# A decoder layer on one core: the key weights of groups 1 and 2 loaded with the initial loads

## The chip, the core and the metric

The kernel runs on one core of a Trainium2 chip. The core has a matrix engine (TensorE, in the profile PE, with its weight loads as PEld), three engines for elementwise work (VectorE or DVE, ScalarE or ACT, GpSimd or POOL) and SyncE (SP), which here only issues DMAs. The engines run side by side; each works through its own instructions in order and waits for others by semaphores. DMAs issued from SP and ACT move data between the chip's memory (HBM) and the on-chip memory (SBUF), or inside SBUF. Matrix products land in PSUM, in banks of 128 x 512 numbers.

The metric is the device time of one execution, in microseconds; the median of several runs counts. All data are 32-bit floats.

## The reference

One layer of a decoder on 1024 tokens of width 512, batch 1. Attention has 32 query heads and 8 key and value heads (groups) of 128 numbers, with rotary position factors and a causal mask; then a feed-forward part of width 1792. Each half is followed by a layer norm.

```python
q, k, v = x @ wq, x @ wk, x @ wv            # 32, 8 and 8 heads of 128
q = q * cos + rotate_half(q) * sin          # k likewise
k, v = repeat(k, 4), repeat(v, 4)           # four query heads share a group
att = softmax(where(causal, q @ k.T / sqrt(128), -inf))
x = layernorm(x + (att @ v) @ wo)
n = x * rsqrt(mean(x * x) + 1e-5) * ln_w
x = layernorm(x + (silu(n @ gate.T) * (n @ up.T)) @ down.T)
```

## The kernel before

**Stages.** A short opening loads x (transposed, in blocks a11, a12, a21, a22), rotary tables and the first weights, and projects the queries and keys of group 0 and the first half of its values. Then eight groups follow, one after the other (`for g in range(KV)`), and last the feed-forward part. In a group the scores of 32 strips of 32 tokens x 4 heads are taken in an order by row tiles of 128 tokens, ORDER = 7, 1, 5, 3, 4, 2, 6, 0. A strip goes through `scores`: products on TensorE into a pair of PSUM banks, mask and lowest value on DVE (L603), exp on ACT (L620), reciprocal on DVE (L624), scaling on ACT (L625), a turn of 32 x 32 blocks on DVE (L628). The part of a strip's tile p that the mask leaves empty is cleared on POOL (L618). When the four strips of a row tile are there, `gather` has SP issue 16 DMAs (L678) that bring the turned blocks into place ("moved<-turned"), and later TensorE multiplies them with the values (tile o).

**What fills the gaps.** Between the scores of group g TensorE does the projections of group g + 1. `steps` is the list of their weights: step 0 is the keys of groups 1 and 2, step 1 queries 4 and 5, step 2 queries 6 and 7, step 3 the values of groups 2 and 3, and so on. `project_two` makes two projections at once by a Strassen-like scheme of seven half-size products; it needs sums of the weight's blocks, which `weigh` makes on POOL (L268 to L270, and one more at L541).

**Loading a step.** `load(s)` issues the DMA of a step's weights on SP (L228), and for keys it adds a scaling of the whole weight on POOL (L236). Step 0 is loaded when the second query head of group 0 has been projected for the second half of the tokens, step 1 after the fourth (in `project_queries`), and step s + 2 at the end of `project_two(s)`. The weights lie in `two_rows`, a pool of four buffers of 128 x 1024; at the start it holds the weights of queries 0 and 1, of queries 2 and 3, and the two parts of the output weight of group 0.

**The queries' buffer.** `held_q` has three places; queries of group g and half `even` lie in place (2g + even) mod 3. Group 0 uses places 0 and 1; place 2 is first written by `project_two(1)`, with the queries of group 1.

**Order.** TensorE's instructions stand in the order in which they are written. On the other engines a planner sets the order by its own estimate of times; `tc.issue_after(ins)` puts an instruction behind another of the same engine. Every DMA on SP also waits for the DMA eight places before it to have landed, since eight semaphores are used in turn.

## Time and profile before

| | |
|---|---|
| runs | 1273.88 us median of 3 (1272.79 to 1274.13) |
| profiled execution | 1272.16 us, span 1270.4 us |
| mean granted TensorE clock | 0.995 of full speed |
| TensorE matmul | busy 1249.0 us, 98% of the span |
| TensorE weight load | busy 737.3 us, 58% |
| DVE | busy 884.4 us, 70% |
| ACT | busy 466.2 us, 37% |
| POOL | busy 469.1 us, 37% |
| DMA queue of SP and ACT | 35.2% of sixteen engines |

How to read the views: a row of a timeline gives start and duration in us, the engine, the line, the operation with its output and input tile, how many instructions are merged, and in brackets the engine's idle time before it and what ended that. SPq is the part of SP that issues DMAs; its row gives the time of issuing, not of the transfer. A row of waits gives the waiting engine, line and tile, who released it, the total in us, how often, and the longest. A row of stretches gives, for a window of the span, the window's length, then each engine's busy time and its number of instructions, the granted TensorE clock (PEclk), the share of DMA engines in use and GB/s. Line L135 is the helper that records every matmul, so matmuls are told apart by their tiles: s scores, o products with the values, q_ps, k_p and q_p projections, y the output projection.

### The profile page before, as it was taken

The numbers are of one execution on the slowest core, as the hardware profiler recorded it, in microseconds if no ns is written. First come the engines' busy times: TensorE is split into PE (matmuls) and PEld (weight loads), VectorE is DVE, ScalarE is ACT, GpSimd is POOL, SyncE is SP. The second block draws the span as 40 slices with busy tenths as digits, with TensorE's granted clock in tenths as the row PEclk, the third lists the DMA queues.
The fourth block names the chain that finished last, engine by engine and source line by source line (L and its number), as shares of the span: only waits on it lengthen the run. The fifth ranks groups of instructions, "written<-read, shape, count | busy, mean of one in ns | idle before, by whom it ended". The sixth has DMA issues, their size and how long they took to land. (4 is left out here: it accounts for less than half of the span.)

```text
span 1270.4 us, 14265 instructions
## 1 busy us (share of the span) xinstructions
PE 1249.0 (98%) x4142; PEld 737.3 (58%) x4142; DVE 884.4 (70%) x1821; ACT 466.2 (37%) x922; POOL 469.1 (37%) x708
## 2 busy tenths in 40 slices
PE   9989999999999999999999999999999999999998
PEld 5644576565556755655567556554656744444887
DVE  4657787788788767878787678687765664436743
ACT  0433344444443444344444444455555111111000
POOL 3442333433434233425341323253320756543321
PEclk9999999999999999999999999999999999999999
DMA  7243225433543344334433433544443711110000
GB/s 257 48 104 91 74 67 136 114 77 80 137 111 86 83 125 98 94 82 119 102 85 85 132 79 81 133 112 111 99 98 90 213 34 50 50 34 1 17 17 34
DMA packets 89326, 115.55 MB, mean 91 GB/s; under 512 B 18464, under 2 KB 60192, under 8 KB 89248
## 3 DMA queue, kind: packets, MB, share of 16 engines
q1 hardware_dynamic: 88240, 112.66, 35.2%
q10 hardware_dynamic: 1008, 1.97, 0.4%
q8 instruction: 34, 0.56, 0.2%
q14 instruction: 44, 0.36, 0.1%
HBM read 37.23 MB, written 2.10 MB: 31 GB/s over the span
## 5 line engine op out<-in xcount | busy, mean ns | idle before, releaser
L620 ACT ACTIVATE p<-s,low 128x928 f32<-128x928 f32 (+31 forms) x256 | 179.0, 699 | 361.5 <-DVE low L603 346.8
L135 PE MATMUL o<-moved,v 128*128 128x512 f32 x550 | 255.1, 597 | 0.0
L628 DVE STREAM_TRANSPOSE turned<-p 128x1024 f32<-128x1024 f32 (+7 forms) x244 | 186.8, 775 | 97.7 <-ACT p L625 62.5
L625 ACT ACTIVATE p<-p,share 128x928 f32<-128x928 f32 (+31 forms) x256 | 187.3, 735 | 121.5 <-DVE share L624 121.5
L603 DVE CUSTOM_DVE_ANT_0 s<-s,mask 128x928 f32<-128x928 f32 (+31 forms) x256 | 179.1, 700 | 63.9 <-PE s L135 63.0
L135 PE MATMUL s<-k,queries 128*128 128x512 f32 (+15 forms) x576 | 204.1, 464 | 2.3 <-ACT p L620 2.3
L135 PEld LDWEIGHTS s<-k,queries 128*128 128x128 f32 x576 | 108.6, 191 | 108.4 <-issue 96.3
L135 PEld LDWEIGHTS o<-moved,v 128*128 128x128 f32 x550 | 102.9, 191 | 104.5 <-issue 98.9
L135 PE MATMUL q_p<-blocks,wq 128*128 128x512 f32 x260 | 123.7, 594 | 0.0
L433 POOL TENSOR_TENSOR queries<-queries,q_b 128x512 f32<-128x512 f32 x52 | 71.0, 1365 | 124.9 <-DVE queries L432 118.5
L618 POOL MEMSET p<- 128x96 f32 (+2 forms) x192 | 26.0, 151 | 213.6 <-DVE turned L628 187.7
L135 PE MATMUL y<-wo,oT 128*128 128x256 f32 x428 | 103.8, 381 | 0.0
L135 PEld LDWEIGHTS y<-wo,oT 128*128 128x128 f32 x428 | 79.8, 190 | 21.5 <-issue 7.4
L427 DVE TENSOR_TENSOR q_b<-queries,sin 64x512 f32<-64x512 f32 x104 | 84.9, 816 | 3.1
L624 DVE RECIPROCAL share<-total 128x1 f32<-128x1 f32 x256 | 39.6, 155 | 56.5 <-ACT p L620 54.3
L135 PEld LDWEIGHTS q_p<-blocks,wq 128*128 128x128 f32 x260 | 48.4, 190 | 46.2 <-issue 40.7
L135 PE MATMUL s<-kT,queries 128*128 128x512 f32 (+8 forms) x192 | 68.4, 467 | 4.7 <-ACT p L620 4.7
L775 DVE TENSOR_TENSOR sums<-y,sums 128x512 f32<-128x512 f32 x112 | 66.9, 607 | 4.4 <-PE y L135 3.5
L135 PE MATMUL y<-u,os 128*128 128x256 f32 x224 | 57.5, 390 | 2.2 <-POOL os L754 2.2
L135 PEld LDWEIGHTS s<-kT,queries 128*128 128x128 f32 x192 | 35.9, 191 | 40.0 <-issue 30.0
L135 PE MATMUL q_p<-blocks,uq 128*128 128x512 f32 x104 | 49.9, 592 | 0.0
L620 ACT ACTIVATION_READ_ACCUMULATOR p<-s,low 128x1 f32 x256 | 49.5, 193 | 0.0
(266 smaller groups left out, 1774.0 us busy)
## 6 DMA issues: line engine op xcount, KB each, us to landing
moved<-turned SPq DMA_DIRECT2D x112, 128.0 KB, 2.4
moved<-turned SPq DMA_DIRECT2D x128, 112.0 KB, 2.2
moved<-turned SPq DMA_DIRECT2D x112, 96.0 KB, 2.1
moved<-turned SPq DMA_DIRECT2D x112, 80.0 KB, 2.1
wo<-wo SPq DMA_DIRECT2D x16, 512.0 KB, 4.1
moved<-turned SPq DMA_DIRECT2D x128, 64.0 KB, 2.0
wq<-wq SPq DMA_DIRECT2D x14, 512.0 KB, 4.2
moved<-turned SPq DMA_DIRECT2D x128, 48.0 KB, 1.9
```

The costliest lines, as they stand in the source:

```text
L135: tc.keep_in_program_order(nc.tensor.matmul(*args, **kw))
L427: nc.vector.tensor_tensor(alike(b[0], dst)[to], dst[of], alike(sin[:, ts], dst)[of], ALU.mult)
L433: nc.gpsimd.tensor_tensor(dst, dst, alike(b[0], dst), ALU.add)
L603: extreme = nc.vector.tensor_tensor_reduce(out=s[:, :n], in0=s[:, :n], in1=mask[:, T - n :], scale=1.0, scalar=MASKED, op0=ALU.add, op1=AL ...
L618: cleared = nc.gpsimd.memset(p[:, n:full], 0.0)
L620: nc.scalar.activation(p[:, :n], s[:, :n], AF.Exp, bias=low, scale=-1.0, accum_out=total)
L624: nc.vector.reciprocal(share, total)
L625: last_of_all = nc.scalar.activation(p[:, :n], p[:, :n], AF.Copy, scale=share)
L628: nc.vector.transpose(x[:, :, :, b, :].rearrange("p b j q -> p j b q"), p[:, :full].rearrange("p (j b k) -> p j b k", b=B, k=Q),)
L775: pin(nc.vector.tensor_tensor(to, out, to, ALU.add))
```

## The change

The weight of step 0, the keys of groups 1 and 2, is no longer loaded by `load(0)` in group 0. Its DMA is issued with the initial loads, behind the second value weight and ahead of the x rows of the residual. It does not go into a buffer of `two_rows` but into place 2 of `held_q`, of which it takes the first 1024 of 2048 numbers of each partition; `held_q` is therefore allocated earlier.

`load_weights` is a generator that stops after the DMA. Its second part, the scaling on POOL, runs when the list of it is exhausted: after the four differences of the query weights at the end of the opening, and behind the last of them on POOL. `weigh(0)` follows there. In `project_queries` the two places that loaded steps 0 and 1 now load steps 1 and 2, and `project_two(0)` loads nothing at its end; from `project_two(1)` on all is as before.

```diff
+        held_q = qp.tile([P, 3, T // 2 // Q, REP, Q], F32, tag="q", name="queries")
...
-            t = (rows if n == 1 else two_rows)(f"w{kind}{which[0]}")
+            if kind == "k" and which == [1, 2]:
+
+                t = held_q[:, 2].rearrange("p n h q -> p (n h q)")[:, :T]
+            else:
+                t = (rows if n == 1 else two_rows)(f"w{kind}{which[0]}")
...
-                nc.gpsimd.tensor_scalar(t, t, -scale, 1.0, ALU.mult, ALU.mult)
+                with tc.issue_after(added.ins) if which == [1, 2] else ExitStack():
+                    nc.gpsimd.tensor_scalar(t, t, -scale, 1.0, ALU.mult, ALU.mult)
...
         list(load_weights("v", [1]))
+        first_keys = load_weights("k", [1, 2])
+        next(first_keys)
         for k in range(NT // 2):
             load_x(k)
...
             if g == 0 and even and head % 2:
-                load(head // 2)
-                if head == REP - 1:
-                    weigh(0)
+                load(head // 2 + 1)
...
-                    load(s + 2)
+                    if s:
+                        load(s + 2)
...
             for a in range(REP):
-                difference(wqs[a])
+                added = difference(wqs[a])
+        list(first_keys)
+        weigh(0)
```

More of the change, by code (lines that the diff above doesn't have):

```diff
@@ L354 @@
         kTs, vs = {}, {}
-        held_q = qp.tile([P, 3, T // 2 // Q, REP, Q], F32, tag="q", name="queries")
         def queries(g, even):
```

## The prediction

> **What bounds the kernel now.** I read the page first: TensorE is busy 1249.0 us of the 1270.4 us span, so only 21.4 us of the run can be won by removing waits; everything else would have to come from fewer matmuls, and the change removes none. Next came the waits of TensorE alone. One of them concerns the tile that the change loads:

> ```profile
> PE k_p L135 <- POOL wk L236: 3.9, 1, 3.9
> ```

> It happens once. The view by stretches shows where, and what follows:

> ```profile
> core 0: us, PE busy (x) PEld busy (x) DVE busy (x) ACT busy (x) POOL busy (x), PEclk, DMA share, GB/s
> 76.90:80.86 3.96, 0.02 (x2) 0.00 (x1) 1.19 (x3) 0.99 (x2) 1.04 (x1) 0.96 0.75 259
> 80.86:84.21 3.35, 3.35 (x4) 1.51 (x5) 0.00 (x0) 0.00 (x0) 3.17 (x5) 0.53 0.00 0
> ```

> TensorE stands still for 3.94 us (76.92 to 80.86), and then its granted clock is 0.53 for 3.35 us. The timeline says what it stood for:

> ```profile
> 75.46 1.45 PE L135 MATMUL s<-kT,queries 128*128 128x512 f32 x4
> ...
> 79.76 1.04 POOL L236 TENSOR_SCALAR wk<-wk 128x1024 f32<-128x1024 f32 x1 [7.24 <-DMA wk<-wk]
> 80.86 0.50 PEld L135 LDWEIGHTS k_p<-blocks,wk 128*128 128x128 f32 x2 [4.34 <-POOL wk L236]
> ...
> 86.63 1.88 PE L135 MATMUL k_p<-blocks,wk 128*128 128x512 f32 x4
> ```

> POOL waits for the DMA of wk, scales the weight for 1.04 us, and TensorE starts at once. Why the DMA is late is in the timeline of the SP queue:

> ```profile
> 55.06 20.35 SPq L678 DMA_DIRECT2D moved<-turned  x32
> 75.52 0.53 SPq L228 DMA_DIRECT2D wk<-wk  x1
> 76.16 0.44 SPq L228 DMA_DIRECT2D wq<-wq  x1
> 86.91 23.83 SPq L678 DMA_DIRECT2D moved<-turned  x32
> ```

> SP issues without a pause from 55.06 to 76.60, some 0.64 us for each of 32 gather transfers, and the key load stands behind them. Its buffer (that of wq 0 and 1) was free when the last projection of query 1 had run, about 58.3. So the bound here is one queue's issue time, not the transfer.

> **The change, part by part.**

> 1. *The key load moves to 14.19* (the SP row of the x loads) and the eight x loads and lnw each go one place back. Cost: 512 KB. The stretch 10 to 20 us moved 351 GB/s, so 1.5 us for whatever lands behind it. Behind it are only x and lnw: cos, the last thing that an engine waits for early (14.39), was asked for at 7.25. No DMA runs from 30 to 40 us (0 GB/s), and the first reader of x is L321 at 35.48. Taken at 0; without that cover 1.5 us.

> 2. *The scaling (1.04) and the three sums of weigh(0) (3 x 0.72)*, 3.2 us of POOL, leave 79.76 to 83.05 and go behind the four differences of wq. In the changed order POOL then does: scaling, clearing of p 28 and 29, sum, clearing of p 30, clearing of sums, two sums, clearing, L321.

> ```profile
> 31.76 2.79 POOL L275 TENSOR_TENSOR wq<-wq 128x256 f32<-128x256 f32 x4
> 34.48 0.34 POOL L618 MEMSET p<- 128x96 f32 x3
> ...
> 35.48 0.74 POOL L321 TENSOR_TENSOR sums<-sums 128x256 f32<-128x256 f32 x1
> 43.27 0.72 POOL L275 TENSOR_TENSOR wv<-wv 128x256 f32<-128x256 f32 x1 [7.05 <-PE v_ps L135]
> ```

> The clearing of p 28 ends at about 34.55 + 1.04 + 0.1 = 35.7; DVE turns that tile at 36.61, so 0.9 us remain. The whole group ends at 36.2 + 3.2 = 39.4, and POOL is next wanted at 43.27. Taken at 0. If the POOL steps ran 1 us longer, DVE's turn would slip by 0.1 us, while TensorE is in matmuls of values (it waits there for exp, not for the turn).

> [...]

> 3. *The stall goes.* After the scores that end at 76.92 TensorE can start the first key product: its bank was last read by DVE at 63.6 (sin products of query 1). Saved: 3.94 us idle. The four passes at low clock took 3.35 us; the same four took 1.71 us from 86.63 to 88.34; saved 1.64. Sum 5.58 us.

> How sure is the 1.64? The trace has two other low stretches, both after shorter waits:

> ```profile
> 872.46:875.87 3.41, 1.09 (x6) 0.64 (x4) 2.21 (x6) 1.26 (x5) 0.18 (x1) 1.00 0.24 58
> 875.87:879.28 3.41, 3.41 (x7) 1.91 (x8) 2.19 (x10) 2.35 (x10) 0.28 (x2) 0.50 0.02 5
> ...
> 903.18:906.59 3.41, 1.54 (x4) 0.47 (x4) 2.86 (x7) 0.57 (x3) 0.12 (x1) 1.00 0.00 0
> 906.59:910.00 3.41, 3.41 (x10) 2.73 (x9) 1.82 (x8) 2.43 (x8) 0.00 (x0) 0.50 0.92 203
> ```

> In a stretch of 3.41 us an idle of 2.32 us, and even 1.87 us, was followed by 3.41 us at half clock. These stretches and the one at 80.57 lie on one grid of 3.413 us (233 and 242 steps apart). A gap of 3.94 us, however it falls on such a grid, leaves at least 1.97 us in one step, over the 1.87 that sufficed. So every execution should pay about half of 3.41 us, and up to some 2.4 when two steps are hit. I take the measured 1.64; bounds 0 and 2.4.

> [...]

> 4. *The loads of queries 4-5 and 6-7 each move one place up*: wq 4 stands at 75.52 where wk stood, wq 6 at 76.16 where wq 4 stood, and the later wq load (110.85) is gone. Count and size on SP stay equal, so nothing is priced. Buffers: those of wq 0 and wq 2, both free by then.

> 5. *What is late next.* TensorE reaches the first product of values for row tile 1 at 84.56 - 5.58 = 78.98; its last gather is issued by 75.41 and such transfers land in 1.9 us, so 77.3: margin 1.7 us. ACT's copy of the first key product, which held back the scaling of p 23 (84.41, then 84.89), comes at about 79.1; the turn of p 23 ends at about 81.7 in place of 86.85, and SP's next gathers start 5.1 us earlier. Their 16 issues at 0.64 and a landing of 2.1 us give 94.1; TensorE wants them (103.0 before) at 97.4: margin 3.3. POOL waits for wq 4 as it waited for wk, to about 79.8, then three sums, the clearing of p 12 (82.1; DVE turns p 12 at about 83.0), the four sums of os, and the last key sum L541 by 86; TensorE wants it at 97.6 - 5.6 = 92. The sums for queries 6-7 come early, at about 87 to 89. None of these reaches TensorE, so from 84.21 on all work moves 5.58 us ahead as one.

> **Against the clock.** The profiled execution took 1272.16 us (span 1270.4 and 1.76 around it): 1272.16 - 5.58 = 1266.6. It lies 1.7 us under the median of the timed runs, 1273.88, and I forecast beside that: **1268.3 us**, 0.44% less.

> **Rivals.**

> - *Only the idle is won.* The clock falls for 3.41 us elsewhere, or did not fall in the timed runs: 1273.88 - 3.94 = 1269.9. For it: a later shift puts the waits at 873 and 904 elsewhere on the grid, where each may cost 1.7 more or less. Against: the rows above. Chance 0.12.
> - *A new wait takes half.* A margin of step 5 is wrong, first that of 1.7 us at the values of row tile 1: one late gather of 1.7 + 2.8 us. 1273.88 - 2.8 = 1271.1, at the edge of no change. Chance 0.06.
> - *The change does not do what it says*: the key product waits at the same place for another thing, a bank or a sum. Then 1273.9. Against: its bank is free at 63.6 and its sums end by 39.4. Chance 0.04.
> - *Slower: POOL is held by wq 4.* POOL now meets the sums of wq 4 first, and the clearing of p 12 stands behind them, behind that DVE's turn of p 12, and DVE's reading of the second key product, whose bank the seventh product needs at 95.9 - 5.6 = 90.3. From landing to that point are 3 x 0.72 + 0.18 + 0.71 + 0.65 = 3.7 us, so TensorE feels a landing after 86.6 (11 us after its issue) and the run becomes slower than before after 92.2 (16.7 us after it). With a landing at 96 it would be 1273.88 + 3.8 = 1277.7. For it: the queue order. Against: 512 KB loads land in 4.2 us, and 7.7 us in the crowd at the start. Chance 0.05.

> **Numbers.** The forecast itself has 0.73; with gains from 3.9 to 7.6 (half-clock price to 2.4, two late waits moving on the grid) it lies at 1266.3 to 1270.0. A change under 0.2% (2.5 us) can't be told from none with this kernel, whose runs spread over 1.3 us. Faster: 0.73 + 0.12 + half of 0.06 = 0.88; same: 0.03 + 0.04 = 0.07; slower 0.05. The range 1266.0 to 1271.3 takes in the first two rivals and leaves out the rest.

> **What would show it.** Right: no wait of TensorE for POOL near 77; granted clock 1.00 from 77 to 84; the key load on SP between the second wv load and x; POOL's scaling near 35; a span near 1264.8. The scores after the key product (84.21 before) should start near 78.6, and any distance kept from there to the end shows step 5. Wrong: TensorE idle before the values of row tile 1 or of row tile 5, DVE waiting for POOL at 36 or 82, or the gain at 100 us given back before the last group ends.

## The result

The changed kernel takes 1267.05 us (median of 4 runs, 1266.03 to 1267.48); the kernel before took 1273.72 us (median of 4, 1272.79 to 1274.13). The recorded ratio is 0.9953, 95% interval 0.9941 to 0.9965. Two later series on the same pair gave 1266.37 against 1272.20 and 1266.54 against 1272.78. The gain is thus 5.8 to 6.7 us by the medians, where 5.6 was forecast. The recorded ratios do not equal the ratios of the medians; in the three series they give 6.0, 5.2 and 6.0 us, each with an interval of 1.5 to 1.8 us to either side. The median lies inside the range of 1266.0 to 1271.3. The profiled execution took 1267.03 us, with a span of 1265.2 us.

**The profile after.** The waits of TensorE no longer have a row for the key product; these are the longest that are left (waiting engine, tile and line, releaser, total in us, times, longest):

```profile
PE s L135 <- ACT p L626: 7.0, 4, 2.3
PE y L135 <- POOL os L760: 1.6, 5, 0.4
PE idle L135 <- DVE turned L362: 1.2, 1, 1.2
PE y L135 <- DVE sums L781: 0.7, 2, 0.5
```

The same two stretches as before, in the changed kernel:

```profile
core 0: us, PE busy (x) PEld busy (x) DVE busy (x) ACT busy (x) POOL busy (x), PEclk, DMA share, GB/s
76.90:80.86 3.96, 3.96 (x11) 1.78 (x10) 2.35 (x6) 2.89 (x6) 0.63 (x1) 1.00 0.82 255
80.86:84.21 3.35, 3.35 (x10) 1.54 (x9) 1.75 (x4) 1.13 (x3) 3.19 (x7) 1.00 0.38 89
```

TensorE is busy through both, at full clock. The timeline there:

```profile
75.36 1.45 PE L135 MATMUL s<-kT,queries 128*128 128x512 f32 x4
...
76.65 1.88 PE L135 MATMUL k_p<-blocks,queries 128*128 128x512 f32 x4
...
79.07 1.88 PE L135 MATMUL o<-moved,v 128*128 128x512 f32 x4
...
82.39 0.18 POOL L624 MEMSET p<- 128x96 f32 x1
...
82.60 0.71 DVE L634 STREAM_TRANSPOSE turned<-p 128x512 f32<-128x512 f32 x1 [1.28 <-POOL p L624]
```

The key product follows the scores at once. Its weight came from the SP queue's opening part, and the gathers of the next row tile start at 81.34 where they started at 86.91:

```profile
14.07 0.80 SPq L236 DMA_DIRECT2D queries<-wk  x1
...
54.95 20.37 SPq L684 DMA_DIRECT2D moved<-turned  x32
75.43 1.07 SPq L236 DMA_DIRECT2D wq<-wq  x2
81.34 42.13 SPq L684 DMA_DIRECT2D moved<-turned  x48
```

Instruction for instruction, TensorE runs 0.10 us ahead of the old profile before the key product, and 5.84 us ahead from the scores after it (78.37 against 84.21) on, so 5.74 us were won there. At the end it is 5.14 us ahead: TensorE waited at two output projections, 0.53 us at 228.9 and 0.22 at 350.6, where the old profile shows no wait.

### The profile page after: what moved, and what is told of

It reads as the page before. It is cut to its first block, busy times and chain, and to the rows that moved or that the text cites. A ratio compares the mean times of both kernels' runs of the same rounds, so it can differ in the third digit from the quotient of the medians.

```text
span 1265.2 us, 14259 instructions
## 1 busy us (share of the span) xinstructions
PE 1247.5 (99%) x4142; PEld 735.9 (58%) x4142; DVE 881.4 (70%) x1821; ACT 466.2 (37%) x922; POOL 471.9 (37%) x708
## 3 DMA queue, kind: packets, MB, share of 16 engines
q10 hardware_dynamic: 1008, 1.97, 0.4%
## 5 line engine op out<-in xcount | busy, mean ns | idle before, releaser
L135 PE MATMUL o<-moved,v 128*128 128x512 f32 x550 | 255.1, 597 | 0.0
L135 PE MATMUL s<-k,queries 128*128 128x512 f32 (+15 forms) x576 | 204.0, 464 | 2.3 <-ACT p L626 2.3
L135 PEld LDWEIGHTS s<-k,queries 128*128 128x128 f32 x576 | 108.5, 191 | 108.5 <-issue 96.3
L135 PEld LDWEIGHTS o<-moved,v 128*128 128x128 f32 x550 | 103.0, 191 | 104.5 <-issue 98.3
L135 PE MATMUL q_p<-blocks,wq 128*128 128x512 f32 x260 | 123.7, 594 | 0.0
L135 PE MATMUL y<-wo,oT 128*128 128x256 f32 x428 | 103.7, 381 | 0.0
L135 PEld LDWEIGHTS y<-wo,oT 128*128 128x128 f32 x428 | 79.8, 190 | 21.5 <-issue 7.8
L434 DVE TENSOR_TENSOR q_b<-queries,sin 64x512 f32<-64x512 f32 x104 | 84.4, 811 | 3.1
L135 PEld LDWEIGHTS q_p<-blocks,wq 128*128 128x128 f32 x260 | 48.4, 190 | 46.3 <-issue 40.5
L135 PE MATMUL s<-kT,queries 128*128 128x512 f32 (+8 forms) x192 | 68.3, 466 | 4.7 <-ACT p L626 4.7
L135 PE MATMUL y<-u,os 128*128 128x256 f32 x224 | 57.5, 390 | 1.6 <-POOL os L760 1.6
L135 PEld LDWEIGHTS s<-kT,queries 128*128 128x128 f32 x192 | 35.7, 190 | 39.7 <-issue 29.2
L135 PE MATMUL q_p<-blocks,uq 128*128 128x512 f32 x104 | 49.8, 592 | 0.0
```

Of the source, the lines that this page charges most:

```text
L135: tc.keep_in_program_order(nc.tensor.matmul(*args, **kw))
L434: nc.vector.tensor_tensor(alike(b[0], dst)[to], dst[of], alike(sin[:, ts], dst)[of], ALU.mult)
```

## The experiments

Each is compared with runs of the kernel before in the same series (median 1272.2 in the first, 1272.36 in the second, 1272.78 in the third); the first series ran on another chip than the other two.

**1. The changed kernel again**, twice, with no edit.

> The changed kernel once more, as the yardstick for the three beside it. Theory (the key weight was late because its DMA stood behind 32 gathers on SP; TensorE lost 3.94 us of idle time and 1.6 to 2.4 us of half clock to it): 1266.0 to 1267.5, as before. In the first profiles 5.74 us were won at the key product, and 0.9 us of them were given back at two output projections (234 and 355 us, TensorE waiting for sums). If those two waits are the change's own doing, they are there again; if they vary from one execution to the next, they are gone or stand elsewhere.

> The changed kernel again, as the yardstick for the two beside it: 1266.4, within 0.7.

Measured: 1266.37 us, ratio 0.9959 (0.9945 to 0.9972), and 1266.54 us, ratio 0.9953 (0.9939 to 0.9967). Between 200 and 400 us neither profile has a wait of TensorE that the view lists, and behind the two places of the waits they are 1.4 and 1.0 us ahead of the first profile. What was given back there belongs to that one execution.

**2. Only the DMA early.** The scaling and the sums stay where they were.

```diff
-        list(first_keys)
-        weigh(0)
...
             if g == 0 and even and head % 2:
+                if head == REP - 1:
+                    list(first_keys)
+                    weigh(0)
                 load(head // 2 + 1)
```

> The DMA stays early, but the scaling on POOL and the sums of weigh(0) go back to where they stood, after the fourth query head (POOL free of the last rotary sum at about 72.4). Theory: scaling ends at 73.5, TensorE wants it at 76.65, so nothing is lost: 1267.0, within 0.7 of the changed kernel. Rival (taking 3.2 us of POOL work out of the way is part of the gain): 1 to 3 us slower than the changed kernel, with TensorE waiting for POOL or DVE for the clearing of p 12.

Measured: 1266.31 us, ratio 0.9952 (0.9940 to 0.9965): the same as the whole change. POOL's timeline shows why: the scaling waits for no DMA and ends at 73.50, 3 us before TensorE wants it (the sums end at 75.8):

```profile
72.45 1.05 POOL L245 TENSOR_SCALAR queries<-queries 128x1024 f32<-128x1024 f32 x1
```

So the time of the DMA is what counts, and moving POOL's 3.2 us adds nothing to it that can be measured.

**3. The readiness of the weight alone, in two doses.** As experiment 2, with further multiplications by 1.0 (n = 4 and n = 7) behind the scaling, so that POOL and not SP makes the weight late.

```diff
                     list(first_keys)
+                    for _ in range(n):
+                        t = held_q[:, 2].rearrange("p n h q -> p (n h q)")[:, :T]
+                        nc.gpsimd.tensor_scalar(t, t, 1.0, 1.0, ALU.mult, ALU.mult)
                     weigh(0)
```

> The early load with POOL's scaling and sums at the old place, and four multiplications of the weight by 1.0 more behind the scaling (1.05 us each). Theory (nothing but the time at which the weight is ready matters): POOL ends them at 72.4 + 5 x 1.05 = 77.7, TensorE wants the weight at 76.65, so 1.05 us are lost and the clock stays: 1.0 us over the changed kernel, 4.8 us under the kernel before. Rival (any wait at this place costs a half-clock stretch): 2.7 us over the changed kernel.

> The same with seven multiplications more: POOL ends at 72.4 + 8 x 1.05 = 80.9, when the key weight was ready in the kernel before, though its DMA is still the early one. Theory: 4.2 us idle and 1.6 to 2.4 us of half clock, so the whole gain is gone: within 0.7 us of the kernel before. Rival (part of the gain comes from the shorter SP queue or the earlier loads of queries 4 to 7): 1 to 3 us under the kernel before.

Measured with four: 1267.85 us, ratio 0.9959 (0.9946 to 0.9971), 4.5 us under the kernel before by the medians; that it is 1 us over the changed kernel, as expected, the intervals can't show. With seven: 1273.51 us, ratio 1.0003 (0.9994 to 1.0012). The waits of TensorE, with four and with seven:

```profile
PE k_p L135 <- POOL queries L488: 1.3, 1, 1.3
```

```profile
PE k_p L135 <- POOL queries L488: 4.7, 1, 4.7
```

Both waits are longer than planned (1.05 and 4.2): the chain ran at 1.1 us a step. With 1.3 us of idle time the clock stayed at 1.00 there; with 4.7 us it was 0.50 for 6.83 us from 80.68 on, twice as long as in the kernel before:

```profile
80.68:84.09 3.41, 2.55 (x3) 1.18 (x4) 0.00 (x0) 0.00 (x0) 3.25 (x5) 0.50 0.01 2
84.09:87.51 3.42, 3.42 (x6) 1.50 (x5) 0.76 (x3) 1.49 (x3) 1.90 (x4) 0.50 0.00 0
```

By the granted 0.50 the 5.97 us of matmuls in it would take half of that at full clock (an estimate), so 3.0 us were lost in this profile, where the prediction had 2.4 as the upper bound. The whole gain was gone, although the load was early and the SP queue short. Nothing else of the change showed a worth: the wait was 0.8 us longer than in the kernel before, and the run is 1.15 us slower by the medians, 0.4 by the ratio (0.8 faster to 1.5 slower).

**4. The price of the low clock alone.** The kernel before, its wait filled with products that count for nothing.

```diff
                 ps[k] = mbank(f"{u}_p{k}")
+                if s == 0 and k == 1:
+                    for _ in range(4):
+                        matmul(ps[k], lhsT=a11[:, 0, :P], rhs=a11[:, 0], start=True, stop=True)
```

> The kernel before with four products more, of x with itself, ahead of the first key product and into its bank (overwritten by it): 4 x 0.86 = 3.4 us of the 3.94 us idle are filled, the load stays as late as it was. Theory (idle time in one step of 3.41 us halves the clock for the next): no low clock near 80, so the price of the low clock alone is won, 1.6 to 2.4 us: 1271.3 to 1272.1. Rival (the low clock is no consequence of this gap, or the timed runs don't pay it): 1273.7.

Measured: 1269.61 us, ratio 0.9981 (0.9973 to 0.9990): 2.6 us by the medians, with the key weight as late as ever. Its stretches:

```profile
76.90:80.86 3.96, 3.53 (x9) 1.26 (x7) 1.70 (x4) 1.93 (x3) 1.04 (x1) 1.00 0.80 262
80.86:84.21 3.35, 3.29 (x8) 1.63 (x9) 1.04 (x3) 0.59 (x1) 3.11 (x6) 1.00 0.38 86
```

The clock is 1.00 in both. The price of the low clock in the timed runs is thus 2.6 us by the medians and 2.4 by the ratio, with an interval of 1.3 to 3.4; this takes in both the 1.64 of the one profile and the prediction's upper bound of 2.4. The mean granted clock, which is listed for every run, says the same from another side: 0.9951 over 45 runs of the kernel before and 0.9969 over 14 of the changed one. By the granted clock of 0.50 half of the time at low clock is lost, which is (1 - clock) x span: 6.24 and 3.89 us, a difference of some 2.3 us (1.7 within the first series, 2.5 within the third; each run's clock is given to three places, so only the means over many runs say this). With the 3.94 us of idle time this makes 6.2 to 6.3 us; 5.8 to 6.7 were measured by the medians. So the price is likely over 1.64, but no run shows it clear of the noise.

**5. The queue alone.** The kernel before, with one load given to ACT's queue.

```diff
-                nc.sync.dma_start(
+                (nc.scalar if kind == "k" and which == [1, 2] else nc.sync).dma_start(
```

> The kernel before with one edit: the DMA of the keys of groups 1 and 2 is issued by ACT's queue, at the same place in the program and into the same buffer as before. Theory: it is issued at about 57.5, when the buffer is free, lands by 62, and the stall goes: 1266.5 to 1268.0. Rival (the buffer, or the transfer beside the gathers, made the load late, not the queue): 1271 to 1274, with TensorE idle near 77. ACT loses some 0.5 us of issue time at 57.5, where it waits for DVE anyway.

Measured: 1269.26 us, ratio 0.9976 (0.9966 to 0.9985), half of the gain. The wait at the key product is gone, so SP's queue was what made the load late. But another has come, for the gathers of row tile 7, at 68.8 us:

```profile
PE o L135 <- DMA moved<-turned: 2.7, 1, 2.7
```

```profile
54.99 5.68 SPq L678 DMA_DIRECT2D moved<-turned  x9
...
57.40 0.39 ACTq L228 DMA_DIRECT2D wk<-wk  x1
...
64.85 4.32 SPq L678 DMA_DIRECT2D moved<-turned  x7
```

SP issued nine gathers, stood from 60.67 to 64.85, and went on; the load, issued at 57.40, took 7.4 us to land, to 64.8. TensorE waited, and the clock fell to 0.50 for 3.41 us from 71.25 on.

**6. Why that cost 2.7 us: one load more amid the gathers**, which nobody reads, in the changed kernel; first behind one gather, then behind six. `scaled` lists ACT's scalings, and its third from the end is that of strip 5; the second run has `exps[-2]`, the exp of strip 6, in its place.

```diff
             if g == 0 and even and head % 2:
+                if head == 1:
+                    more = held_q[:, 2].rearrange("p n h q -> p (n h q)")[:, T:]
+                    with tc.issue_after(scaled[-3].ins):
+                        nc.scalar.dma_start(
+                            more.rearrange("p (c f) -> p c f", c=NC),
+                            wk[:, HD : 3 * HD].rearrange("(c p) f -> p c f", p=P),
+                        )
                 load(head // 2 + 1)
```

> The changed kernel with one load more that nobody reads: the same 512 KB of the key weight once again, issued by ACT at the place of the load in the run with ACT's queue (about 56 us, amid the 32 gathers), into the idle half of place 2 of the queries' buffer. It tells why that run won only half. Theory (a 512 KB transfer amid the gathers delays them: there SP stopped for 4.2 us, and TensorE waited 2.7 us for the gathers of row tile 7): the same wait here, with its half clock, 2.5 to 4.4 us over the changed kernel. Rival (that run lost because of its buffer, its scaling on POOL at 65 us or its order): no wait at 69 us, within 0.7 us of the changed kernel.

> The run with one more load that nobody reads, issued later: behind exp of strip 6 on ACT, at about 58.8, so behind six gathers and not one. The theory that any transfer amid the gathers costs the 2.7 us has fallen (0.4 us there). New theory: SP stops because its DMAs take eight semaphores in turn with the loads of ACT, and the gather whose turn it is waits until the load has landed; there the load landed at 60.9, 0.9 us after the turn came, with ACT's queue at 64.8, 4.2 us after. Here the turn comes with the eleventh gather, about 61.3, and the load lands 5.6 to 7.4 us after its issue, at 64.4 to 66.2: SP stops for 3 to 5 us, TensorE waits 1.5 to 3.5 us for row tile 7, and with its half clock the run is 1.5 to 5 us over the changed kernel. Rival (the buffer or POOL's scaling made that wait): no more than 0.7 us over it.

Measured, behind one gather: 1266.77 us, ratio 0.9954 (0.9941 to 0.9966), the same as the changed kernel's 0.9959 and 0.9953. Its wait and SP's rows:

```profile
PE o L135 <- DMA moved<-turned: 0.4, 1, 0.4
```

```profile
54.96 5.04 SPq L693 DMA_DIRECT2D moved<-turned  x8
...
60.92 8.31 SPq L693 DMA_DIRECT2D moved<-turned  x13
```

The theory that any such transfer holds the gathers up by 4 us fell here. Behind six gathers: 1268.12 us, ratio 0.9963 (0.9950 to 0.9976), 1.6 us over the changed kernel beside it by the medians, with intervals that overlap:

```profile
55.16 6.42 SPq L692 DMA_DIRECT2D moved<-turned  x10
...
58.50 0.40 ACTq L487 DMA_DIRECT2D queries<-wk  x1
...
63.84 5.57 SPq L692 DMA_DIRECT2D moved<-turned  x9
```

```profile
PE o L135 <- DVE queries L417: 0.8, 1, 0.8
```

In the three runs SP resumed at 64.85, 60.92 and 63.84, and the load landed at 64.83, 60.91 and 63.82. So SP stood until the load had landed and went on 0.01 to 0.02 us after it, each time with a gather that waits for the semaphore of that very load (in the traces 108, 108 and 100). How long SP stands depends on when the turn comes: 60.67 (5 gathers after the load), 60.00 (7 after it), 61.58 (4 after it). The semaphore is not the whole of it, since gathers behind the load also landed late: in experiment 5 the gather issued at 57.55 landed at 64.64, after 7.1 us, where the one issued at 57.60 in the kernel before landed after 2.5. No run separates the two. The stop of 2.3 us is under the 3 to 5 expected, since the load landed in 5.3 us; the wait of TensorE was 0.8 us and its clock stayed at 1.00. The view puts this wait down to DVE's L417, which ended at 69.59; but the last gather of row tile 7 landed at 69.33, 2.3 us later than in the changed kernel, where the same product began before that DVE step had ended. Of the 1.6 us the profile accounts for 1.0 at 69.7; the rest stays open.

**7. The same low clock elsewhere.** Two products into an unread bank ahead of three late scores, first at places that I had read wrongly, then, with strips 1, 6 and 1, at the right ones.

```diff
             s = pair(f"s{u}")
+            if (g, t) in ((KV - 2, 17), (KV - 1, 6), (KV - 1, 17)):
+                fill = mbank(f"fill{u}")
+                for _ in range(2):
+                    matmul(fill, lhsT=kT[:, :P], rhs=kT[:, :W], start=True, stop=True)
```

> The changed kernel with two products into an unread bank (2 x 0.86 us) ahead of each of three score products of the last two groups, which wait 2.3, 1.9 and 2.2 us for ACT (at 869, 899 and 970 us of the changed kernel). Theory (idle time of about 1.9 us and more in one step of the 3.41 us grid halves the clock for the next step, which costs 1.7 us, and the profile of the changed kernel pays that twice): no low clock there, 1.5 to 3.4 us under the changed kernel, 1263 to 1265 where that takes 1266.4. Rival (the low clock there is not due to the idle time, or costs nothing because ACT sets the pace): within 0.7 us of the changed kernel, or slower if a bank is not free for the fill.

> The run with filled waits again, with two of the three places mended: there the fill stood ahead of scores that do not wait (833 and 934 us) and cost 1.57 and 1.82 us, and only the one at 899 us met its wait. Now the fills (2 x 0.86 us) stand ahead of the second strip of row tile 0 in the last two groups and of the third strip of row tile 1 in the last. Theory (idle time over about 1.9 us in a step of the grid halves the clock for the next): waits of 2.3, 1.9 and 2.2 us shrink to under 0.6, no low clock at 870 and 900, and the run is 1.5 to 3.4 us under the changed kernel: 1263.0 to 1264.9. Rival (no price): within 0.7 us of it.

First run: 1269.01 us, slower than the changed kernel by some 2.5 us (it was not run again in this series). The row "s 128x64" at 870 us is the second strip of row tile 0 (64 columns in all), not the end of strip 17 (512 + 64 columns); two fills stood where nothing waits and cost some 1.7 us each. Second run: 1263.31 us, ratio to the kernel before 0.9925 (0.9912 to 0.9938), and 3.2 us under the changed kernel beside it (1266.54). This version beats both kernels. Its waits of scores for ACT:

```profile
PE s L135 <- ACT p L630: 1.7, 4, 0.6
```

Its stretches, and those of the changed kernel at the same work:

```profile
868.40:871.80 3.40, 2.88 (x10) 1.43 (x9) 1.81 (x11) 2.58 (x6) 0.00 (x0) 1.00 0.09 19
871.80:875.20 3.40, 3.40 (x11) 1.65 (x10) 2.05 (x9) 2.33 (x10) 0.55 (x4) 1.00 0.42 95
896.00:899.40 3.40, 3.25 (x9) 1.31 (x8) 2.85 (x6) 0.66 (x3) 0.13 (x1) 1.00 0.00 0
899.40:902.80 3.40, 3.40 (x16) 2.64 (x15) 1.73 (x8) 2.42 (x8) 0.00 (x0) 1.00 0.96 212
```

```profile
867.64:871.06 3.42, 1.10 (x6) 0.72 (x5) 2.20 (x6) 1.31 (x4) 0.18 (x1) 1.00 0.24 57
871.06:874.47 3.41, 3.41 (x8) 1.86 (x9) 2.18 (x10) 2.42 (x9) 0.28 (x2) 0.50 0.02 5
898.36:901.78 3.42, 1.55 (x5) 0.53 (x4) 2.87 (x6) 0.65 (x3) 0.12 (x1) 1.00 0.00 0
901.78:905.19 3.41, 3.41 (x10) 2.75 (x9) 1.74 (x8) 2.43 (x8) 0.00 (x0) 0.50 0.95 210
```

The scores still come when ACT lets them; only the waiting is spent on products, and the 3.4 us of two low stretches are won.

## Why the prediction was right, point by point

- *What bounds the kernel* (the key load behind 32 gathers on SP): shown. With the load early the wait goes (experiment 2), with the load on another queue the wait at this place goes (5), and with the weight late for another reason the whole gain goes (3).
- *Step 1, the load at the start, taken at 0*: right. It was issued at 14.07. Up to the key product the runs differ by 0.10 us, and in favour of the change.
- *Step 2, POOL's 3.2 us at 34.5, taken at 0*: right. POOL's timeline after the change:

```profile
34.51 1.05 POOL L245 TENSOR_SCALAR queries<-queries 128x1024 f32<-128x1024 f32 x1
...
38.68 0.73 POOL L330 TENSOR_TENSOR sums<-sums 128x256 f32<-128x256 f32 x1
43.16 0.72 POOL L284 TENSOR_TENSOR wv<-wv 128x256 f32<-128x256 f32 x1 [3.76 <-PE v_ps L135]
```

  It ends at 39.4, as worked out, and 3.76 us of idle time are left of 7.05. DVE's turn at 36.50 and mask at 37.67, beside POOL's sums, took 1.25 and 1.13 us, as in the kernel before (36.61 and 37.77), where POOL was idle. Other steps of the two engines did take longer side by side. In the kernel before DVE's L1008 took 1.21 us while POOL was idle (at 52.66) and 2.09 beside POOL's L412, clearings and L321 (at 58.16). In the changed kernel DVE's L434, which took 0.69 us while POOL was idle (at 96.22), took 1.04 beside POOL's L278, at the sums for queries 6 and 7, and that step 1.05 us in place of the 0.73 at 36.84:

```profile
88.32 1.04 DVE L434 TENSOR_TENSOR k_b<-k,sin 64x512 f32<-64x512 f32 x1
...
88.89 1.05 POOL L278 TENSOR_TENSOR uq<-wq,uq 128x256 f32<-128x256 f32 x1
```

```profile
895.29:898.70 3.41, 1.54 (x5) 0.47 (x4) 2.86 (x7) 0.48 (x2) 0.12 (x1) 1.00 0.00 0
898.70:902.11 3.41, 3.41 (x15) 2.67 (x16) 1.95 (x9) 2.42 (x7) 0.00 (x0) 1.00 0.87 192
```

  A gap of 3.94 us leaves at least 1.97 in one step, which fits the conclusion that nearly every execution pays. One step that is itself at half clock does not fit these counts: the one from 80.68 in experiment 3 had only 0.86 us of idle time, and half clock went on behind it. Counted as work at full clock, at the granted 0.50, its 2.55 us of matmuls are 1.28, which leaves 2.1 us without work; counted so, the other 22 steps at half clock leave 1.7 to 1.85, and full clock came behind each. This reading rests on one step, and no run tests it. A step need not be idle throughout: in the changed kernel those from 867.64 and 898.36, with 1.10 and 1.55 us of matmuls, were followed by 3.41 us at 0.50 (experiment 7).
- *Step 5, what is late next*: right in its main numbers. The values of row tile 1 began at 79.07 (78.98 forecast) without a wait; gathers started at 81.34 (81.7); POOL's last key sum ended at 86.6 (86). One row was not foreseen in its size: DVE waited 1.28 us for the clearing of p 12, which wq 4 held back (its sums began at 80.23, 79.8 forecast). The prediction had named DVE waiting for POOL at 82 as a sign of being wrong; the sign came, and the gain was there all the same, so it was a poor sign. The wait is the mechanism of the slower rival; it cost TensorE nothing, since by the prediction TensorE would feel a landing only after 86.6, and wq 4 landed at 80.17.
- *Against the clock*: the profiled execution came to 1267.03 where 1266.6 was worked out, and the median to 1267.05 where 1268.3 was forecast. Taking over the profile's distance of 1.7 us from the median did not help: the later series put the kernel before at 1272.2 to 1272.8, so the profiled execution was not low, and in the profiled pair, which differ by 5.13 us, the sum was right to 0.5 us.
- *Rivals*: only the idle won (1269.9) and the new wait (1271.1) did not come. The new wait is real when the load goes amid the gathers (2.7 us in experiment 5), which this change avoids by going ahead of them.

## What to carry to other kernels

A late load is first a question of what stands ahead of it on its issuing queue: here 32 issues of 0.64 us each kept a 512 KB load back for 17 us after its buffer was free, and a piece of buffer idle from the start let it go ahead of them all. Moving it to another queue amid that traffic may only move the wait: in experiments 5 and 6 SP stood 4.2, 0.9 and 2.3 us, until the load on ACT's queue, whose semaphore it took next, had landed, and a gather behind the load took 7.1 us to land in place of 2.5. And a wait of TensorE of 2 us or more within one step of the grid costs more than its length in these profiles: add the half clock of the stretch behind it (3.41 us at 0.50, which cost 1.6 to 2.6 us here), or fill the wait with products that nobody reads.

## What the runs showed that was not expected

- Single runs of one kernel differ mostly with their mean granted clock: over 45 runs of the kernel before, time and clock have a correlation of -0.83. The profile of experiment 2 had no low stretch before the last product and took 1263.26 us, where its other four runs took 1265.89 to 1267.69, with the same program.
- Two unread products ahead of each of three scores that waited about 2 us took two stretches of half clock away and won 3.2 us (experiment 7), half as much as the change itself; the waits left before scores came to 1.7 us in place of 7.0.
- A 512 KB load amid gathers took 5.3 to 7.4 us to land, against 4.1 behind them (in the kernel before, issued at 75.52 and used at 79.76).
